# The MLP's three products by Strassen's scheme of seven half products, in a two-block transformer kernel

## The chip, the cores and the metric

One Trainium2 chip, one core of it, all numbers in float32. The time is the device time of one execution, in microseconds; each kernel is compared by the median of its runs. The engines are called PE (matrix products; PEld is its weight loads), DVE, ACT, POOL (elementwise work) and SP (here only the issue of DMAs).

## What is computed

Two blocks over x of 32 sequences x 64 tokens x 512 channels, conditioned on one vector of 512 per sequence:

```
block 0: h = rms(x) * (w1 * (1 + cond @ tw1.T));   q, k, v = h @ Wq.T, h @ Wk.T, h @ Wv.T   (8 heads of 64, one k and v)
         x += softmax(rope(q) rope(k).T / 8) v @ Wo.T
         h = rms(x) * (w2 * (1 + cond @ tw2.T))
         x += (silu(h @ Wg.T) * (h @ Wu.T)) @ Wd.T          Wg, Wu: 2048 x 512, Wd: 512 x 2048
block 1: h = layernorm(x) * (1 + scale) + shift;  q = h @ Wq.T (16 heads of 32);  c = h @ Wkd.T (128)
         k, v = c @ Wku.T, c @ Wvu.T (4 groups);   x += softmax(masked rope(q) rope(k).T / sqrt(32)) v @ Wo.T
```

The change concerns the line with Wg, Wu and Wd.

## The kernel before

All activations lie transposed: 128 channels on the partitions, tokens in the free dimension. The 2048 tokens are cut into 8 units of 256 (4 sequences). A unit passes through `attention0` (first block's attention and the norm for the MLP), `mlp`, and `attention1` (the whole second block, which also writes the result). `mlp(g)` works on a group of two units, 512 tokens. It loops over 16 blocks f of 128 hidden channels: 4 matmuls for gate, 4 for up (line 687, each 128x128 weights by 512 columns), Silu on ACT (692), the product `act` on DVE (695), and one block later 4 matmuls of down into four banks (678). At the end DVE adds the four banks to x (704). The weights of a block f (gate, up and down, 768 KB) come by one DMA into one of four `mw` buffers and are loaded anew in each of the four groups; `load_chunks` asks for block f + 4 when down has used block f.

Each of these functions is a Python generator. It yields after every piece with two numbers, a guess of PE's time and of the time until its next piece can go on. `Order.run` picks, among the jobs that can go on, the one with the least share done, so that attention's pieces stand between the MLP's in PE's instruction stream; a list scheduler then fixes the order on each engine. Every engine works its own stream in order and waits there by semaphores, SP's stream of DMA issues too. While `mlp(g)` runs, attention0 of the next two units and attention1 of earlier ones are interleaved. The last two units' attention1 run at the end, with every PSUM bank to themselves. PSUM has eight banks of 512 columns: two `at` for attention, two `gu` for gate and up, four `acc` for down.

Other steps that are spoken of: `rotate` (371 to 374, rotary embedding: three DVE products, one POOL addition), `softmax` (381 to 388), `turned` (394, transposes on PE), `inverse_root` (332 and 333: Sqrt on ACT, reciprocal on DVE), `rms` (324, 325 and 349 on POOL), `angles` (253 to 282, positions to sines and cosines on DVE).

Of the kernel before, what the change touches and what calls it, by code (L numbers as in the profile page):

```python
# [10 lines left out]
F32 = mybir.dt.float32  # L11
# [13 lines left out]
GT = 512  # L25
NG = T // GT
FF = 2048
NF = FF // P
# [64 lines left out]
def two_blocks(ctx: ExitStack, tc: tile.TileContext, a: dict, out: bass.AP):  # L93
# [3 lines left out]
    wk = ctx.enter_context(tc.tile_pool(name="wk", bufs=2))  # L97
    psum = ctx.enter_context(tc.tile_pool(name="psum", bufs=2, space=PSUM))
# [69 lines left out]
    XB = NU - 1  # L168
# [7 lines left out]
    chunks = {}  # L176

    def load_chunks(upto):

        for j in range(len(chunks), min(upto, NG * NF)):  # L180
            t = work("mw", [P, 3, 512], f"mw_{j}", MW)
            nc.sync.dma_start(t, a["wmlp"][j % NF])
            chunks[j] = t
# [3 lines left out]
    def load_mod(i):  # L187

        if i < 2:
            t = work("h2", [P, KC, D], f"mod_{i}", 2)  # L190
            nc.sync.dma_start(t, a["mod"][i])
            mods.append([t[:, :, c * P : (c + 1) * P] for c in range(KC)])
            return
        mods.append([])
        for j in range(2):
            t = work("mw", [P, KC, D // 2], f"mod_{i}_{j}", MW)
            nc.sync.dma_start(t, a["mod"][i][:, :, j * 256 : (j + 1) * 256])
            mods[i] += [t[:, :, c * P : (c + 1) * P] for c in range(2)]
# [3 lines left out]
    posi = work("pT", [P, GT], "posi", 3).bitcast(I32)  # L202
    nc.sync.dma_start(posi, a["pos"])
# [4 lines left out]
    load_mod(2)  # L208
    load_mod(3)
    load_x(2)  # L210
    load_x(3)


    def modulation(i):
# [12 lines left out]
        rows = work("latT", [P, UT], f"rows_{i}", 1)[:, :P]  # L227
# [16 lines left out]
    def angles(u0, u1):  # L244
        cols = slice(u0 * S, u1 * S)

        def room(tag, name, bufs):
            return work(tag, [P, 512], f"{name}_{u0}", bufs)[:, : (u1 - u0) * S]

        posf, sign = room("u", "posf", 2), room("v", "sign", 2)  # L250
        ang, lo, hi, prod = (room("p", n, 4) for n in ("ang", "lo", "hi", "prod"))
        acc, rnd = angle[:, 0, cols], angle[:, 1, cols]
        nc.vector.tensor_copy(posf, posi[:, cols])
# [28 lines left out]
        nc.vector.tensor_tensor(rnd, rnd, sign, ALU.mult)  # L282

    def tables(u, r):
# [6 lines left out]
        cs = work("cs", [P, 2, UT], f"cs_{u}", 2)  # L291
# [17 lines left out]
    RING = {"h": 4, "p": 4, "pT": 3, "sq": 1, "latT": 1, "kr": 1}  # L309

    def space(room, tag, columns, name):

        if room is not None and tag in room:
            return room[tag].pop(0)[:, :columns]
        return work(tag, [P, columns], f"{name}", RING.get(tag, 2))

    def mean_of(t, lean, name):

        if lean:
            ps = abank(name)  # L320
            for k in range(KC):
                nc.tensor.matmul(ps[:, :UT], ones, t[:, k], start=(k == 0), stop=(k == KC - 1))
        else:
            nc.gpsimd.tensor_tensor(t[:, 0:2], t[:, 0:2], t[:, 2:4], ALU.add)
            nc.gpsimd.tensor_tensor(t[:, 0], t[:, 0], t[:, 1], ALU.add)
            yield 0.0, 3.5
            ps = abank(name)
            nc.tensor.matmul(ps[:, :UT], ones, t[:, 0], start=True, stop=True)
        return ps[:, :UT]
# [5 lines left out]
    def rms(u, s, h, lean, name):  # L335

        x = x_units[u]
        sq = work("h" if lean else "sq", [P, KC, UT], f"sq_{name}", 4 if lean else 1)
        nc.scalar.activation(sq, x, AF.Square)
        if lean:  # L340
            c = KC // 2
# [6 lines left out]
        else:  # L348
            nc.gpsimd.tensor_tensor(by_seq(h), by_seq(x), per_seq(s, u), ALU.mult)  # L349
        ps = yield from mean_of(sq, lean, f"ms_{name}")  # L350
        r = work("r", [P, UT], f"r_{name}", 2)
        inverse_root(ps, eps0, r)
# [6 lines left out]
    def rotate(dst, src, cos, sin, shape, name, room=None):  # L359
# [4 lines left out]
        u, v = (space(room, tag, 512, f"{tag}_{name}") for tag in "uv")  # L364
# [11 lines left out]
    def softmax(sc, scale, name, p):  # L376
# [3 lines left out]
        mx = work("mx", [P, 8], f"mx_{name}", 3)  # L380
# [4 lines left out]
        sm = work("sm", [P, 8], f"sm_{name}", 3)  # L385
# [26 lines left out]
    h2s = {}  # L412

    def attention0(u, lean=False, early=None):
        g = u // 2
        half = slice((u % 2) * UT, (u % 2 + 1) * UT)
        kb, vb = kblk0[u % 2], vblk0[u % 2]
        h = work("h", [P, KC, UT], f"h0_{u}", 4)
        norm = rms(u, s0a, h, lean, f"a{u}")
# [8 lines left out]
        qT = work("qT", [P, KC, UT], f"qT0_{u}", 2)  # L428
# [55 lines left out]
        for t in range(2):  # L484
# [12 lines left out]
            ps.append(softmax(sc, HD0**-0.5, f"0_{u}_{t}", space(None, "p", 512, f"p0_{u}_{t}")))  # L497
            yield 1.0, 5.0 * t

        cT = work("h", [P, KC, UT], f"cT0_{u}", 4)  # L500
        for t in range(2):
            pT = turned(ps[t], f"0_{u}_{t}", space(None, "pT", 512, f"pT0_{u}_{t}")).rearrange("p (c t) -> p c t", c=KC)
# [17 lines left out]
        if u % 2 == 0:  # L520
            h2s[g] = work("h2", [P, KC, GT], f"h2_{g}", 2)
        h = h2s[g][:, :, half]
        r = yield from rms(u, s0b, h, lean, f"b{u}")
        nc.vector.tensor_tensor(h, h, all_chunks(r), ALU.mult)  # L524
        yield 0.43, 0.0


    def attention1(u, room=None):
        vb = room["vb"] if room else vblk1[u % 2]
        x = x_units[u]  # L530
        lean = room is not None and "h" in room

        def tile4(tag, name):
            return space(room, tag, KC * UT, name).rearrange("p (c t) -> p c t", t=UT)

        h = tile4("h", f"h1_{u}")
        if lean:
            mean = yield from mean_of(x, True, f"mean_{u}")
        else:
            sums = tile4("sq", f"sum_{u}")  # L540
            nc.gpsimd.tensor_tensor(sums[:, 0:2], x[:, 0:2], x[:, 2:4], ALU.add)
            nc.gpsimd.tensor_tensor(sums[:, 0], sums[:, 0], sums[:, 1], ALU.add)
            yield 0.0, 3.5
            mean = abank(f"mean_{u}")[:, :UT]
            nc.tensor.matmul(mean, ones, sums[:, 0], start=True, stop=True)
        nc.vector.tensor_tensor(h, x, all_chunks(mean), ALU.subtract)
        sq = tile4("sq", f"sq1_{u}")
        nc.scalar.activation(sq, h, AF.Square)  # L548
        nc.gpsimd.tensor_tensor(by_seq(h), by_seq(h), per_seq(s1, u), ALU.mult)  # L549
        yield 0.43, 3.0  # L550
        var = yield from mean_of(sq, lean, f"var_{u}")
        r = space(room, "r", UT, f"r_c{u}")
        inverse_root(var, eps1, r)
# [10 lines left out]
        qT = tile4("qT", f"qT1_{u}")  # L564
        cos, sin = cs1[:, 0, :], cs1[:, 1, :]

        def query(i):
            q = abank(f"q1_{u}_{i}")
            for c in range(2):
# [9 lines left out]
                room,  # L579
# [7 lines left out]
        for t in range(2):  # L587
# [12 lines left out]
            room,  # L600
        )
        kb = space(room, "kb1", KC * UT, f"kb1_{u}").rearrange("p (b g s) -> p b g s", b=US, g=NKV1)
# [16 lines left out]
        cT = tile4("h", f"cT1_{u}")  # L619
# [51 lines left out]
    def mlp(g):  # L671
        h = h2s[g]
        accs = [bank("acc", f"down_{g}_{c}") for c in range(KC)]

        def down(f, act):
            w = chunks[g * NF + f][:, 2]
            for c in range(KC):
                nc.tensor.matmul(accs[c], w[:, c * P : (c + 1) * P], act, start=(f == 0), stop=(f == NF - 1))  # L678
            load_chunks(g * NF + f + 1 + MW)

        before = None
        for f in range(NF):
            w = chunks[g * NF + f]
            gate, up = bank("gu", f"gate_{g}_{f}"), bank("gu", f"up_{g}_{f}")
            for ps, i in ((gate, 0), (up, 1)):
                for k in range(KC):
                    nc.tensor.matmul(  # L687
                        ps, w[:, i, k * P : (k + 1) * P], h[:, k, :], start=(k == 0), stop=(k == KC - 1)
                    )
                if i == 0:  # L690
                    sg = work("sg", [P, GT], f"sg_{g}_{f}", 2)
                    nc.scalar.activation(sg, gate, AF.Silu)  # L692
                yield 3.4, 0.0
            act = work("act", [P, GT], f"act_{g}_{f}", 3)
            nc.vector.tensor_tensor(act, sg, up, ALU.mult)  # L695
            if before is not None:
                down(*before)
                yield 3.4, 0.0
            before = f, act
        down(*before)  # L700
        for i in range(2):
            x = x_units[2 * g + i]
            for c in range(KC):
                nc.vector.tensor_tensor(x[:, c], x[:, c], accs[c][:, i * UT : (i + 1) * UT], ALU.add)
        yield 3.4, 0.0


    A0, A1, M = 24.0, 24.0, 164.0
    order = Order()

    def first(u, rank=0):
        return Job(attention0(u), A0, rank)

    def second(u, rank=0):
        return Job(attention1(u), A1, rank)

    def other_mods():
        for i in range(1, 4):
            yield from modulation(i)

    def after(*jobs):

        for j in jobs:
            yield from j

    def early():
        angles(0, 2)
        for z in (kblk0[0], vblk0[0], kblk0[1], vblk0[1], *vblk1):
            nc.gpsimd.memset(z, 0.0)
# [129 lines left out]
```

## Time and profile before

| | |
|---|---|
| median of 3 runs | 1123.04 us (1122.53 to 1123.87) |
| profiled execution | 1121.74 us, its span 1119.9 us |
| mean granted PE clock | 0.986 of full speed |
| first MLP matmul | 95.1 us after the span's start |
| last MLP matmul | 1011.6 us |
| PE / DVE / ACT / POOL busy | 96 / 36 / 24 / 20 % of the span |
| DMA | 68.8 MB, 61 GB/s on average |

The span is the time between the first and the last instruction. A line of the groups reads: source line, engine, operation, what is written from what, shapes and count, then busy time in us, mean duration in ns, and after the second bar the engine's idle time just before and what ended it. A matmul's duration is its latency from start to result; matmuls in a row overlap, so its price on PE is the distance between two starts. In the timeline the columns are start, time until the last of the merged instructions ended, engine, line, operation, and count.

### The profile page before, as it was taken

To read this page: it belongs to the slowest core of one execution; us is meant where nothing else is said; L and a number is where in the kernel's file an instruction comes from. 1 tells how busy PE (TensorE), PEld (TensorE's weight loads), DVE (VectorE), ACT (ScalarE), POOL (GpSimd) and SP (SyncE) were. 2 spreads that over 40 slices of the span, in tenths; PEclk is the share of its full clock that TensorE was granted. 3 is DMA by queue.
4 is the path that set the end of the run, shared out by engine and by line. 5 is a ranking of instruction groups with operands and counts; after the bars stand their busy time and mean duration, and the time that the engine had idled before them with its cause. 6 is when DMAs were issued, how large, how long until landed. Compare 5 with 4: busy or idle time off the path is not lost.

```text
span 1119.9 us, 10307 instructions
## 1 busy us (share of the span) xinstructions
PE 1079.6 (96%) x4100; PEld 631.6 (56%) x4100; DVE 407.2 (36%) x722; ACT 266.5 (24%) x441; POOL 226.5 (20%) x197
## 2 busy tenths in 40 slices
PE   6789999999999999999999999999999999999796
PEld 5575455645464645465565655555554555546584
DVE  5884111432252144332433224322233023115543
ACT  2231021121212142412114221243023023113222
POOL 2311012111132120202322212202131022014431
PEclk9899999999999999999999999999999999999898
DMA  9500211111201111112101121101111111200000
GB/s 363 220 1 1 85 56 57 57 57 56 85 29 56 57 57 57 57 65 84 59 28 57 37 67 57 57 29 66 66 57 57 75 56 57 75 1 0 1 30 29
DMA packets 16271, 68.83 MB, mean 61 GB/s; under 512 B 1632, under 2 KB 3936, under 8 KB 15456
## 3 DMA queue, kind: packets, MB, share of 16 engines
q1 hardware_dynamic: 16224, 68.17, 17.3%
q8 instruction: 33, 0.54, 0.2%
q14 instruction: 14, 0.11, 0.0%
HBM read 63.97 MB, written 4.19 MB: 61 GB/s over the span
## 4 chain that ended last, share of the span: by engine, by line
PE 89%; DVE 7%; POOL 1%; issue 1%; ACT 1%; DMA 0%; SPq 0%; ACTq 0%; DVEq 0%; POOLq 0%
PE down L678 20%; PE gate L687 19%; PE up L687 19%; PE po L357 9%; PE q L357 8%; PE sc L625 2%; PE pp L394 2%; PE cx L646 1%; PE lat L357 1%; PE sc L490 1%; PE cx L506 1%; PE kv L357 1%; PE tab L288 1%; DVE mx L381 1%; DMA mod<-in_mod 0%
## 5 line engine op out<-in xcount | busy, mean ns | idle before, releaser
L687 PE MATMUL up<-h,mw 128*128 128x512 f32 x512 | 232.8, 595 | 0.0
L678 PE MATMUL down<-act,mw 128*128 128x512 f32 x512 | 232.2, 595 | 0.0
L687 PE MATMUL gate<-h,mw 128*128 128x512 f32 x512 | 231.6, 594 | 0.4 <-DVE h L524 0.4
L687 PEld LDWEIGHTS gate<-h,mw 128*128 128x128 f32 x512 | 95.8, 190 | 107.8 <-issue 105.5
L678 PEld LDWEIGHTS down<-act,mw 128*128 128x128 f32 x512 | 95.6, 190 | 107.3 <-issue 105.4
L687 PEld LDWEIGHTS up<-h,mw 128*128 128x128 f32 x512 | 95.2, 190 | 108.0 <-issue 107.0
L695 DVE TENSOR_TENSOR act<-sg,up 128x512 f32<-128x512 f32 x64 | 43.7, 682 | 291.3 <-PE up L687 282.3
L692 ACT ACTIVATE sg<-gate 128x512 f32<-128x512 f32 x64 | 38.2, 597 | 315.0 <-PE gate L687 276.0
L357 PE MATMUL po<-cT,wo 128*128 128x256 f32 x448 | 100.8, 379 | 0.7 <-ACT cT L515 0.7
L357 PEld LDWEIGHTS po<-cT,wo 128*128 128x128 f32 x448 | 84.9, 190 | 21.2 <-issue 9.5
L388 POOL TENSOR_TENSOR p<-p,sm 128x512 f32<-128x512 f32 x40 | 41.2, 1042 | 234.0 <-DVE sm L387 225.8
L374 POOL TENSOR_TENSOR qT<-u_q,v_q 128x512 f32<-128x512 f32 x28 | 35.5, 1267 | 170.9 <-DVE v_q L373 170.9
L407 DVE TENSOR_TENSOR x<-x,po 128x512 f32<-128x512 f32 x32 | 22.0, 687 | 117.4 <-PE po L357 117.4
L357 PE MATMUL q<-h,wqkv 128*128 128x256 f32 x256 | 59.6, 384 | 1.6 <-DVE h L346 1.6
L381 DVE TENSOR_REDUCE mx<-sc 128x8 f32<-128x512 f32 x48 | 32.8, 685 | 75.6 <-PE sc L625 53.6
L357 PEld LDWEIGHTS q<-h,wqkv 128*128 128x128 f32 x256 | 48.6, 192 | 12.3 <-issue 5.8
L692 ACT ACT_TABLE_LOAD x30 | 38.5, 1283 | 59.6 <-PE gate L687 59.4
L357 PE MATMUL q<-h,wq 128*128 128x256 f32 x192 | 43.5, 379 | 0.1
L357 PEld LDWEIGHTS q<-h,wq 128*128 128x128 f32 x192 | 36.3, 190 | 6.6 <-issue 1.7
L384 ACT ACTIVATE p<-p 128x512 f32<-128x512 f32 x40 | 24.8, 629 | 54.7 <-DVE p L383 54.6
L549 POOL TENSOR_TENSOR h<-h,s 128x1024 f32<-128x1024 f32 x6 | 11.4, 1901 | 123.5 <-ACT sq L548 123.5
L349 POOL TENSOR_TENSOR h<-x,s0b 128x1024 f32<-128x1024 f32 x6 | 11.4, 1902 | 122.8 <-DVE x L407 122.8
(190 smaller groups left out, 1038.9 us busy)
## 6 DMA issues: line engine op xcount, KB each, us to landing
mw<-in_wmlp SPq DMA_DIRECT2D x64, 768.0 KB, 4.3
x<-in_x SPq DMA_DIRECT2D x8, 512.0 KB, 9.4
out_x<-x SPq DMA_DIRECT2D x16, 256.0 KB, 2.0
mod<-in_mod SPq DMA_DIRECT2D x2, 1024.0 KB, 8.4
wo<-in_wo SPq DMA_DIRECT2D x2, 1024.0 KB, 13.0
mod<-in_mod SPq DMA_DIRECT2D x4, 512.0 KB, 14.4
wqkv<-in_wqkv SPq DMA_DIRECT2D x1, 1280.0 KB, 9.0
wq<-in_wq SPq DMA_DIRECT2D x1, 1024.0 KB, 11.4
```

Of the source, the lines that this page charges most:

```text
L357: nc.tensor.matmul(ps, w[:, k, cols], h[:, k, :], start=(k == 0), stop=(k == KC - 1))
L374: nc.gpsimd.tensor_tensor(dst, cut(u, every), cut(v, every), ALU.add)
L381: nc.vector.tensor_reduce(mx, s3, AX.X, ALU.max)
L384: nc.scalar.activation(p, p, AF.Exp, scale=scale)
L388: nc.gpsimd.tensor_tensor(p3, p3, sm.unsqueeze(2).to_broadcast(heads), ALU.mult)
L394: nc.tensor.transpose(pp[:, c, :], p[:, c * P : (c + 1) * P], ident)
L407: nc.vector.tensor_tensor(x[:, part], x[:, part], po, ALU.add)
L625: nc.tensor.matmul(sc[b * S : (b + 1) * S, j * 256 : (j + 1) * 256], qT[:, 2 * h_ + j, cols], kb[:, 2 * t + b].rearrange("p g k -> p (g k) ...
L678: nc.tensor.matmul(accs[c], w[:, c * P : (c + 1) * P], act, start=(f == 0), stop=(f == NF - 1))
L687: nc.tensor.matmul(ps, w[:, i, k * P : (k + 1) * P], h[:, k, :], start=(k == 0), stop=(k == KC - 1))
L692: nc.scalar.activation(sg, gate, AF.Silu)
L695: nc.vector.tensor_tensor(act, sg, up, ALU.mult)
```

## The change

A product C = A B is cut into a 2 x 2 grid of blocks on each side. Instead of eight block products, seven are formed of sums of blocks (Winograd's form of Strassen's scheme), and their sums give the four blocks of C.

- The MLP runs unit by unit (256 tokens, in halves of `HT` = 128), and over `NP` = 8 pairs of hidden blocks, 256 channels: 64 steps. In each step gate, up and down each form P1 to P7, of two 128x128 by 128-column matmuls.
- The weight side of one product is a set of seven slots of 128x256: three blocks as they are (slots 4 to 6) and four sums (slots 0 to 3). In the first unit `combine` forms the sums, three operations on POOL and one on DVE, and `done_with` stores them to `kept`, 24 tiles in HBM. In later units slots 0 to 3 are loaded from there. There are four set buffers; a set is loaded when the set four places before it is used up.
- The token side is formed on chip: `attention0` adds four DVE operations for sums of h (`hc`); `gated` forms act and its sums (`td`) on POOL.
- `first_products` puts four of the products into the quarters of one `gu` bank; ACT copies one out, DVE adds three times; `last_products` accumulates the other three on top of the quarters that were read, and DVE adds once more. Silu is made in two parts. For down the seven sums stand in the four `acc` banks over all eight steps, and are added to x at the unit's end.
- Buffers: 5 x tiles for 7; the attention's buffers in two named sets (`ring`); the smaller buffers shared or single; positions loaded two units at a time.
- The order: the MLP starts when unit 0 is ready; attention0 of the next unit and a chain of attention1 of units 0 to 5 run beside it; units 6 and 7 at the end.

The core of the diff:

```diff
+    OF = {"P1": (4, "B11"), "P6": (1, "T2"), "P5": (0, "T1"), "P7": (2, "T3")}
+    OF |= {"P2": (5, "B21"), "P3": (3, "B22"), "P4": (6, "T4")}
...
+            t = work("mw", [P, 7, 2 * P], f"set_{n}", MW)
+            nc.sync.dma_start(t[:, 4:7], a["wmlp"][i][:, 0:3])
+            if q < NP:
+                odd[n] = work("a21", [P, 2 * P], f"a21_{n}", 2)
+                nc.sync.dma_start(odd[n], a["wmlp"][i][:, 3])
+            else:
+                nc.sync.dma_start(t[:, 0:4], kept[i])
...
+            nc.gpsimd.tensor_tensor(t[:, 0], a21, t[:, 6], ALU.add)
+            nc.gpsimd.tensor_tensor(t[:, 1], t[:, 0], t[:, 4], ALU.subtract)
+            nc.vector.tensor_tensor(t[:, 2], t[:, 4], a21, ALU.subtract)
+            nc.gpsimd.tensor_tensor(t[:, 3], t[:, 5], t[:, 1], ALU.subtract)
...
+    def done_with(m, q):
+        n = place[m, q]
+        if q < NP:
+            nc.sync.dma_start(kept[3 * (q % NP) + m], sets[n][:, 0:4])
+        load_sets(n + 1 + MW)
...
+        nc.vector.tensor_tensor(t1_, b12, b11, ALU.subtract)
+        nc.vector.tensor_tensor(b12, b22, b12, ALU.subtract)
+        nc.vector.tensor_tensor(t2_, b22, t1_, ALU.subtract)
+        nc.vector.tensor_tensor(t4_, b21, t2_, ALU.subtract)
...
-            gate, up = bank("gu", f"gate_{g}_{f}"), bank("gu", f"up_{g}_{f}")
-            for ps, i in ((gate, 0), (up, 1)):
-                for k in range(KC):
-                    nc.tensor.matmul(
-                        ps, w[:, i, k * P : (k + 1) * P], h[:, k, :], start=(k == 0), stop=(k == KC - 1)
-                    )
...
+        for i, p in enumerate(("P1", "P6", "P5", "P7")):
+            product(ps[:, i], p, w, b, start=i == 0)
+        e = work("e", [P, HT], f"e_{m}_{q}")
+        nc.scalar.copy(e, ps[:, 0])
+        u2 = work("u2", [P, HT], f"u2_{m}_{q}")
+        nc.vector.tensor_tensor(u2, e, ps[:, 1], ALU.add)
+        w2 = work("w2", [P, HT], f"w2_{m}_{q}")
+        nc.vector.tensor_tensor(w2, u2, ps[:, 2], ALU.add)
+
+        c = work("gate" if m == 0 else "up", [P, 4, HT], f"c_{m}_{q}", 2 - m)
+        nc.vector.tensor_tensor(c[:, 2], w2, ps[:, 3], ALU.add)
...
+        for i, p in ((0, "P2"), (2, "P3"), (3, "P4")):
+            product(ps[:, i], p, w, b, stop=p == "P4")
+        nc.vector.tensor_tensor(
+            c.rearrange("p (a b) t -> p a b t", b=2)[:, :, 1],
+            ps[:, 2:4],
+            u2.unsqueeze(1).to_broadcast([P, 2, HT]),
+            ALU.add,
+        )
+        done_with(m, q)
...
+        nc.vector.tensor_tensor(act[:, 0], gate[:, 0], ps[:, 0], ALU.mult)
+        nc.gpsimd.tensor_tensor(act[:, 1:4], gate[:, 1:4], c[:, 1:4], ALU.mult)
+        td = work("td", [P, 4, HT], f"td_{q}")
+        nc.gpsimd.tensor_tensor(td[:, 0:2], act[:, 1:3], act[:, 0:2], ALU.subtract)
+        nc.gpsimd.tensor_tensor(td[:, 2], act[:, 2], td[:, 0], ALU.subtract)
+        nc.gpsimd.tensor_tensor(td[:, 3], act[:, 3], td[:, 2], ALU.subtract)
...
+            gate = first_products(0, q)
+            yield 1.8, 0.0
+            up = first_products(1, q)
+            yield 1.8, 0.0
+            before = down(q - 1) if q else iter(())
+            yield from before if q == 0 else (next(before),)
+            last_products(0, q, *gate)
+            nc.scalar.activation(gate[2][:, 0], gate[0][:, 0], AF.Silu)
+            nc.scalar.activation(gate[2][:, 1:4], gate[2][:, 1:4], AF.Silu)
+            yield 1.3, 0.0
+            last_products(1, q, *up)
+            gated(q, up[0], up[2], gate[2])
+            yield 1.3, 0.0
+            for _ in before:
+                pass
```

## The prediction, made before the changed kernel was run

> **What bounds the kernel now.** I read the page first: busy times, slices, the chain that ended last, the costliest groups and the DMA issues.
>
> ```profile
> span 1119.9 us, 10307 instructions
> ...
> PE 1079.6 (96%) x4100; PEld 631.6 (56%) x4100; DVE 407.2 (36%) x722; ACT 266.5 (24%) x441; POOL 226.5 (20%) x197
> ...
> PE 89%; DVE 7%; POOL 1%; issue 1%; ACT 1%; DMA 0%; SPq 0%; ACTq 0%; DVEq 0%; POOLq 0%
> ...
> L687 PE MATMUL up<-h,mw 128*128 128x512 f32 x512 | 232.8, 595 | 0.0
> L678 PE MATMUL down<-act,mw 128*128 128x512 f32 x512 | 232.2, 595 | 0.0
> L687 PE MATMUL gate<-h,mw 128*128 128x512 f32 x512 | 231.6, 594 | 0.4 <-DVE h L524 0.4
> ...
> mw<-in_wmlp SPq DMA_DIRECT2D x64, 768.0 KB, 4.3
> ```
>
> PE is 89% of the chain; the three MLP products have almost no idle time before them. Each 128-row product in float32 stands in the trace as two matmuls: 256 by the program per product, 512 by the profile. So PE's own time is what must shrink. "595" is one matmul's latency; the price is the distance from one start to the next, and the timeline gives it.
>
> ```profile
> 105.52 3.60 PE L687 MATMUL up<-h,mw 128*128 128x512 f32 x8
> 105.52 0.19 PEld L687 LDWEIGHTS up<-h,mw 128*128 128x128 f32 x1 [0.24 <-issue]
> ```
>
> Eight matmuls of 512 columns take (3.60 - 0.595)/7 = 0.429 us each; the weight load of 0.19 us hides under them. MLP now: 1536 x 0.429 = 659 us. The change makes columns few and loads many, so I looked for 128 columns with a new weight block each time.
>
> ```profile
> 66.96 1.04 PE L394 MATMUL pp<-ident,p 128*128 128x128 f32 x8
> ```
>
> ```profile
> 356.19 0.63 PEld L588 LDWEIGHTS kv<-wkv,latT 128*128 128x128 f32 x4
> 356.41 0.61 PE L588 MATMUL kv<-wkv,latT 128*128 128x128 f32 x4
> ```
>
> These come from the timeline; 0.273 and 0.275 are the latencies in the tiles' rows. The transposes: (1.04 - 0.273)/7 = 0.110 us. The kv product: (0.61 - 0.275)/3 = 0.112 us, its four loads starting at the same pace although each lasts 0.19 us. So loads follow one another at 0.11 us, and 128 columns cost just over a quarter of 512 (0.107).
>
> Last, from the groups by shape, POOL's and then DVE's, the prices of the engines that get new work (the number before the last bar is the mean in ns).
>
> ```profile
> L324 POOL TENSOR_TENSOR sq_b<-sq_b 128x512 f32<-128x512 f32 x6 | 7.6, 1265 | 0.0
> ...
> L325 POOL TENSOR_TENSOR sq_b<-sq_b 128x256 f32<-128x256 f32 x6 | 4.3, 723 | 0.5
> ```
>
> ```profile
> L704 DVE TENSOR_TENSOR x<-x,down 128x256 f32<-128x256 f32 x32 | 12.0, 418 | 4.8 <-PE down L678 3.6
> ...
> L264 DVE TENSOR_TENSOR prod<-prod,angle 128x128 f32<-128x128 f32 x16 | 4.7, 292 | 0.5
> ```
>
> **PE's work.** Per unit (256 tokens) and pair of blocks (a "step", 64 in all) there are 3 products x 7 half products x 2 matmuls = 42, in the trace 84. All: 64 x 84 = 5376. At 0.110 that is 591 us, at 0.112 602; I take 0.111: 597, a gain of 62 us (57 to 68). A step is 84 x 0.111 = 9.32 us in six pieces: gate's and up's first four products (1.78 each), down's first four of the step before (1.78), then gate's, up's and down's last three (1.33 each).
>
> The Trainium skill, page "TensorE: Matmul & The Clock Gate", section "Back-to-back issue gap", speaks against this: streams of load and matmul at 128 columns are paced at about 81 ns where the matmul alone would take about 56. Scaling 0.110 by 81/56, an estimate from that page, makes MLP 855 us and the kernel about 1346. The rows above, with a new weight block for every matmul, show no such factor; no row here shows more than eight in a row.
>
> **Evictions, units 1 to 7.** MLP's 0.68 us DVE product per f goes (64, 44 us). A step gets on DVE seven operations of 128 columns (0.29) and two of 256 (0.42): 2.9 us, 184 us in all; DVE comes to some 570 of 1090 us, not a bound. ACT gets two small copies and the Silu in two parts, about 1.3 us a step, plus six table loads by the order of instructions (79 for 73, 1.28 us each); off the path. POOL gets act (384 columns, 0.99 between its 256 and 512 rows) and td (0.72 + 2 x 0.45): 2.6 us, 167 in all.
> What counts is each wait of PE against its cover:
> - Gate's last products need four readings of its first (copy 0.27, three adds 0.87, hand-overs and matmul latency 0.4): 1.55 us; up's and down's first products cover 3.56. Up's: the same 1.55 under 3.11.
> - Down needs act and td: latency and add 0.7, POOL until the second operand of down 1.0 + 0.72 + 0.45: 2.9 us, under down's rest, gate's and up's first products, 4.89.
> - The gate and up banks come free in 0.7 to 1.0 us, under 2.67 and 3.11.
> So alone nothing shows. Attention's operations stand in the same queues: on DVE runs of 2 us (rotate, three at 0.69) to 4.7 (reciprocal of line 333 1.75, h of line 524 1.28, four new sums at 0.42), on ACT a table load and Exp, on POOL 1.0 (line 388) to 1.9 (line 349) each. They use up the spare 1.5 to 2 us, but bring PE work that widens it: before, MLP ran from 95 to 1012 us, 917 us with 659 of MLP, so 258 of attention (about 4 us a step). I take 0.2 us a step: 56 x 0.2 = 11 us. Below: zero. Above: 1.65 us a step, see the slower rival.
>
> **Unit 0, where sums are made.** Here POOL also has three operations of 256 columns for each of three sets a step: 9 x 0.723 = 6.5, with act and td 9.1 us beside PE's 9.32, and hardly any attention widens it (only the rest of unit 1's first block). Its queue takes act and td first (0.6 for the add and hand-overs, then 2.6), then up's, down's, gate's sums. The next up's second product needs two sums (2 x 0.723 = 1.45): they end 3.2 + 1.45 = 4.7 us after the last up, PE is there after 1.33 + 1.78 + 0.44 = 3.55; so it waits 1.15, and down's sums add some 0.35. So 1.5 us x 8 = 12 us. SP adds a queue of its own: a set's load waits behind the store of the previous set's sums, and that behind POOL. Below: 0, if the order turns out kinder. Above: DMA's price, next. From the timeline of POOL and then of DVE, a contended operation (start, duration):
>
> ```profile
> 525.97 1.67 POOL L325 TENSOR_TENSOR sq_a<-sq_a 128x256 f32<-128x256 f32 x1
> ```
>
> ```profile
> 525.85 1.21 DVE L524 TENSOR_TENSOR h<-h,r_b 128x1024 f32<-128x1024 f32 x1
> ```
>
> 1.67 for 0.72, beside a DVE operation with both inputs in SBUF. DVE's slot 2 of each set is of that kind.
>
> **DMA.** Before, 64 loads of 0.79 MB. Now a set is 0.92 MB (0.39 weights, 0.52 kept sums), three a step: 2.75 MB; in unit 0 loads of 0.52 and stores of 0.52, 3.15 MB. Four buffers: up's set is asked for when gate's is used up, 4.4 us of PE work ahead, down's 6.2, gate's 12. The window 20 to 30 us moved 396 GB/s:
>
> ```profile
> 20.00:30.00 10.00, 10.00 (x64) 8.62 (x57) 7.70 (x23) 3.21 (x5) 1.17 (x1) 1.00 1.06 396
> ```
>
> At that rate 2.75 MB take 6.9 us of a 13 us step: hidden; the first product of a set uses raw weights, so kept sums may land 0.45 later. At the lone load's 0.79 MB in 4.3 us (183 GB/s, nothing overlapped) a step takes 15 us, 1.7 more than the 13.3 there is: 95 us over 56 steps, and in unit 0 17.2 us for 9.3, 63 us. The three loads are asked for within 2.7 us of one another, like the window's queued loads, so I take the upper rate and nothing beyond unit 0's 12. SP's two loads a set cost 0.33 us each of issue (one x load's issue in the timeline); behind out_x and the three later x loads sets can wait 2.0 us (out_x's landing): 0 to 6, taken as 0.
>
> **Boundaries, head, end.** Eight units instead of four groups: four evictions of DVE and the four sums end later than PE wants; 7 x 0.7 = 5 us (0 to 20). MLP starts after one unit, near 75 us instead of 95, but the attention work that stood there comes later: 0 (-5 to +5). The end keeps two and a half second blocks: 0 (-5 to +5).
>
> **The sum**, against the profiled execution's 1121.7 us (span 1119.9 and 1.8 around it): -62 + 11 + 12 + 5 = -34, so 1087.7. That execution lies 1.3 below the median of 1123.0; added, 1089.
>
> **Rivals.**
> *All hidden.* No wait is added: 1123 - 68 = 1055 to 1061. For it: every cover above exceeds its chain. Against: unit 0's POOL is full.
> *Slower: POOL's queue.* Place: down's wait for td. Attention has about 170 us of POOL in MLP's stretch, 2.7 us a step; with one h operation of 1.9 that itself waits for a reciprocal of 1.75, the chain of 2.9 grows to 6.55 and misses 4.89 by 1.66: 56 x 1.65 = 92, with the 17 of unit 0 and the boundaries 1123 - 62 + 92 + 17 = 1170. It decides from 45/56 = 0.8 us a step with the other terms as they are. Against: attention's PE work widens 4.9 to about 7.
> *Loads pace PE.* If a long stream needed the whole 0.19 of a load, MLP takes 1021 us and the kernel 1485; the 0.11 pace of four loads speaks against it.
>
> **Chances.** Forecast, waits of 15 to 50 us in all, so 1076 to 1111: 0.52. All hidden: 0.26. POOL's queue, in any strength: 0.19 (of it 0.14 past the break-even). Loads: 0.03. What this kernel's measurement can tell from no change is 0.2%, 2.2 us. Faster 0.79, within 0.04, slower 0.17. The range 1054 to 1140 leaves out the worst of POOL's queue and the loads.
>
> **What would show it.** In the profile after: 128-column MLP matmuls, eight or more together, at 0.110 to 0.112; if nearer 0.19, I am wrong at the root. PE's idle time in unit 0 about 12 us, released by POOL's sums or DMA; afterwards short waits of down for td and of last products for DVE adds. If SPq or DMA releases PE in units 1 to 7, the lone rate was right. If PE idles over 60 us in all that the before does not have, it is slower.

## The result, and the profile after

The changed kernel takes 1128.11 us (median of 4 runs, 1127.75 to 1129.35), the kernel before 1122.78 in the same comparison: ratio 1.0050, 95% interval 1.0032 to 1.0067. It is slower by half a percent, where 3% less was forecast. The page of the changed kernel, busy times, chain and the MLP's groups:

```profile
span 1126.0 us, 20184 instructions
...
PE 1045.3 (93%) x7940; PEld 954.6 (85%) x7940; DVE 577.9 (51%) x1314; ACT 317.6 (28%) x647; POOL 471.2 (42%) x557
...
PE 69%; DVE 11%; POOL 7%; DMA 5%; ACT 3%; issue 2%; SPq 0%; POOLq 0%; ACTq 0%; DVEq 0%
...
L719 PE MATMUL gu<-h,set 128*128 128x128 f32 x2048 | 293.4, 278 | 9.8 <-ACT c L814 3.7
...
L719 PE MATMUL gu<-hc,set 128*128 128x128 f32 x1536 | 217.0, 277 | 11.9 <-POOL set L212 7.8
...
L778 PE MATMUL down<-td,set 128*128 128x128 f32 x1024 | 137.4, 277 | 5.9 <-POOL set L212 3.3
```

PE fell from 96 to 93% busy, its share of the chain from 89 to 69%: DVE, POOL and DMA took the rest. The MLP's groups had next to no idle time before them; now they have. PE's waits, from the view of waits (us in all, times, longest):

```profile
PE lat L400 <- POOL h L599: 9.9, 5, 4.6
PE pp L437 <- POOL p L431: 9.0, 8, 6.7
PE gu L719 <- POOL set L212: 7.8, 6, 1.6
PE tab L325 <- DVE angle L317: 7.4, 3, 4.1
...
PE gu L719 <- ACT c L814: 3.7, 5, 1.5
PE gu L719 <- DVE hc L570: 3.3, 4, 1.4
PE down L778 <- POOL set L212: 3.3, 4, 2.0
PE gu L719 <- DVE c L738: 2.6, 3, 1.2
```

No wait dominates; it is a long list, and that view leaves short ones out. So for all kernels I also added up, from the trace, the distance from each matmul's start to the next beyond what its columns take when nothing waits (0.109 us for 128 columns, 0.216 for 256, 0.429 for 512). "Head" is before the first MLP matmul, "tail" after the last, both without the time before PE's first matmul; a constant excess below 0.01 us a matmul, 13 us in all at 128 columns, is kept apart. The kernels below "changed" are the experiments of the next section.

| kernel | median us | ratio to before, 95% | head | unit 0 | units 1 to 7 | tail |
|---|---|---|---|---|---|---|
| before | 1122.8 | | 24.8 | 13.9 for all units | | 25.8 |
| changed | 1128.1 | 1.0032 to 1.0067 | 30.3 | 23.0 | 60.2 | 16.9 |
| conv | 1129.2 | 1.0049 to 1.0086 | 25.8 | 0.0 | 28.0 | 13.1 |
| convcut | 1052.8 | 0.9341 to 0.9396 | 26.2 | 0.0 | 35.0 | 15.4 |
| bare | 1092.7 | 0.9718 to 0.9747 | 26.8 | 5.3 | 45.0 | 17.2 |
| nosum | 1109.1 | 0.9865 to 0.9916 | 26.7 | 7.9 | 59.6 | 17.3 |
| nodma | 1121.4 | 0.9988 to 1.0012 | 31.2 | 22.2 | 56.1 | 17.3 |
| notd | 1121.8 | 0.9966 to 1.0020 | 28.1 | 19.0 | 55.4 | 17.3 |
| noadd | 1133.4 | 1.0063 to 1.0148 | 28.9 | 20.6 | 69.4 | 20.1 |
| noangle | 1120.6 | 0.9962 to 1.0009 | 29.0 | 23.8 | 53.7 | 17.3 |
| ownsilu | 1127.9 | 1.0027 to 1.0067 | 28.8 | 24.1 | 63.8 | 17.3 |
| lag | 1123.6 | 1.0000 to 1.0018 | 27.6 | 26.0 | 56.5 | 17.0 |
| tddve | 1118.4 | 0.9968 to 1.0004 | 28.2 | 17.9 | 53.5 | 17.0 |
| tddvelag | 1118.4 | 0.9931 to 0.9989 | 30.5 | 16.5 | 57.8 | 17.3 |
| plain0 | 1134.9 | 1.0104 to 1.0161 | 27.9 | 19.1 | 65.4 | 20.1 |
| plain0b | 1129.8 | 1.0044 to 1.0075 | 27.7 | 13.3 | 64.1 | 16.8 |
| combo | 1118.3 | 0.9956 to 0.9985 | 27.2 | 12.4 | 55.8 | 16.9 |
| store | 1136.6 | 1.0075 to 1.0146 | 31.9 | 28.2 | 60.7 | 17.3 |
| best2 | 1127.6 | 1.0022 to 1.0055 | 34.0 | 24.9 | 56.6 | 16.9 |
| dvesum | 1109.4 | 0.9863 to 0.9903 | 27.6 | 10.0 | 53.4 | 17.3 |

Waits are those of one profiled execution, and executions of several kernels differ by up to 12 us, so a difference of a few us between two rows of waits says little. The kernel before took 1121.1 to 1122.8 us beside the several experiments, so medians of two rows can differ by 1 to 2 us for nothing. From before to changed: products 659 to 600.6, so 58 us less, and waits 64.5 to 130.4, so 66 more. That is the result: the products shrank as forecast, and PE stood still for all of it and a little more.

### The profile page after: what moved, and what is told of

The parts are those of the page before. It is cut to its first block, busy times and chain, and to the rows that moved or that the text cites. A ratio compares the mean times of both kernels' runs of the same rounds, so it can differ in the third digit from the quotient of the medians.

```text
span 1126.0 us, 20184 instructions
## 1 busy us (share of the span) xinstructions
PE 1045.3 (93%) x7940; PEld 954.6 (85%) x7940; DVE 577.9 (51%) x1314; ACT 317.6 (28%) x647; POOL 471.2 (42%) x557
## 4 chain that ended last, share of the span: by engine, by line
PE 69%; DVE 11%; POOL 7%; DMA 5%; ACT 3%; issue 2%; SPq 0%; POOLq 0%; ACTq 0%; DVEq 0%
PE gu L719 25%; PE down L778 13%; PE po L400 10%; PE q L400 8%; DMA set<-sums 3%; DMA set<-in_wmlp 2%; PE sc L667 2%; PE lat L400 2%; PE pp L437 2%; PE cx L547 1%; PE kv L400 1%; PE sc L531 1%; PE cx L688 1%; POOL set L212 1%; POOL set L211 1%
## 5 line engine op out<-in xcount | busy, mean ns | idle before, releaser
L719 PE MATMUL gu<-h,set 128*128 128x128 f32 x2048 | 293.4, 278 | 9.8 <-ACT c L814 3.7
L719 PEld LDWEIGHTS gu<-h,set 128*128 128x128 f32 x2048 | 262.2, 193 | 23.0 <-issue 11.3
L719 PE MATMUL gu<-hc,set 128*128 128x128 f32 x1536 | 217.0, 277 | 11.9 <-POOL set L212 7.8
L719 PEld LDWEIGHTS gu<-hc,set 128*128 128x128 f32 x1536 | 194.0, 193 | 15.2 <-POOL set L212 8.9
L757 POOL TENSOR_TENSOR act<-c,c 128x384 f32<-128x384 f32 x64 | 65.0, 1015 | 218.0 <-DVE c L745 174.5
L778 PE MATMUL down<-td,set 128*128 128x128 f32 x1024 | 137.4, 277 | 5.9 <-POOL set L212 3.3
L778 PEld LDWEIGHTS down<-td,set 128*128 128x128 f32 x1024 | 125.2, 192 | 9.4 <-POOL set L212 4.1
L778 PE MATMUL down<-act,set 128*128 128x128 f32 x768 | 110.2, 278 | 1.0 <-DMA set<-in_wmlp 0.8
L745 DVE TENSOR_TENSOR c<-gu,u 128x256 f32<-128x256 f32 x128 | 53.5, 421 | 112.0 <-PE gu L719 111.0
L778 PEld LDWEIGHTS down<-act,set 128*128 128x128 f32 x768 | 98.7, 193 | 7.6 <-issue 3.6
```

Of the source, the lines that this page charges most:

```text
L719: nc.tensor.matmul(ps, w[:, slot, k * P : (k + 1) * P], b[of][:, k], start=start and k == 0, stop=k == 1, skip_group_check=True)
L745: nc.vector.tensor_tensor(c.rearrange("p (a b) t -> p a b t", b=2)[:, :, 1], ps[:, 2:4], u2.unsqueeze(1).to_broadcast([P, 2, HT]), ALU.add,)
L757: nc.gpsimd.tensor_tensor(act[:, 1:4], gate[:, 1:4], c[:, 1:4], ALU.mult)
L778: nc.tensor.matmul(sums_of[u][p][:, c], w[:, slot, c * P : (c + 1) * P], b[of], start=q % NP == 0 and i % 2 == 0 and c == 0, stop=q % NP = ...
```

## The experiments

The edits are shown shortened.

### What each part of the change is worth

**conv**: the changed kernel's units, buffers and order, with plain products and plain evictions. **nosum**: no sums of weights formed or stored.

```diff
+ for r in range(2): for k in range(KC): matmul(ps[:, r], w[:, SLOT[r, k // 2], ...], h[:, k, :])     # conv
+ activation(sg, gate, Silu); tensor_tensor(act, sg, up, mult)
+ nc.sync.dma_start(t[:, 0:4], a["wmlp"][i])                                                          # nosum
- combine(...); dma_start(kept[...], sets[n][:, 0:4])
```

> The changed kernel's frame (units of 256 tokens, its order, its buffers, its set loads) with plain products of 256 columns: no sums, no evictions by quarters. MLP's products cost 64 x 48 x 0.216 = 663 us for 602, so +61 at equal waits. Theory A (the waits come from the elementwise work that Strassen adds): the waits of units 1 to 7 fall from 60 to 15 to 25 us and those of unit 0 from 23 to under 5, in all about -60: 1120 to 1135 us. Rival C (they come from the rest of the change: order by unit, single buffers): the waits stay, 1165 us or more. Rival B (late sets): the loads are 0.52 MB for 0.92, so this one does not tell B from A.

> Leaves out the forming and storing of the sums: slots 0 to 3 are loaded from the weights in every unit, so the values are others; every other instruction stays. Theory A: unit 0's waits of 23 us, released by POOL's sums, go; about 1128 - 20 = 1108, units 1 to 7 unchanged within 4 us. Rival B (DMA): unit 0 now loads 0.92 MB a set as the others do, waits stay near 15 to 20 us, released by DMA: 1122 or more.

**bare** takes away, beyond nosum, the elementwise operations that the scheme adds in every step. What stays of the scheme are the sets of 0.92 MB (conv's are 0.52) and, at the end of each unit, down's sums (one operation on ACT, seven on DVE, four on POOL, where conv has four on DVE). **convcut** takes one matmul of eight from conv.

```diff
- u2, w2, c, hc and td sums, second Silu                     # bare, on top of nosum
+ activation(gate[2], gate[0], Silu); tensor_tensor(act, gate, ps, mult)
- for k in range(KC):                                        # convcut, on top of conv
+ for k in range(KC - r):
```

> Seven half products in the same order as in the changed kernel, but none of the elementwise work that the scheme adds: no sums of weights (all sets are loaded), of tokens or of act, and gate and up are evicted as plain ones are, one Silu and one product of the whole bank (the outputs are not the reference's). It stands against the kernel without sums of weights, 1109.1. Theory A (the added elementwise work makes the waits): units 1 to 7 fall from 60 us of waits to the 28 of plain products, unit 0 from 8 to 0: 1109 - 40 = 1069 (1062 to 1078). Theory D (PE has less MLP work to cover attention's chains, whatever stands beside it): waits stay, 1095 to 1108.

> Plain products and plain evictions in the changed kernel's frame, with one of eight matmuls of every block left out (the outputs are not the reference's): 663 x 1/8 = 83 us less MLP work on PE and nothing added elsewhere; it stands against plain products, 1129.2. Theory A: the waits stay near the 28 us of plain products: 1129 - 83 = 1046 (1042 to 1054). Theory D: with less to lay under attention's chains PE waits 25 to 40 us more in units 1 to 7: 1070 to 1086. Between them: both count.

Measured: conv 1129.2 and nosum 1109.1, both where theory A had them, bare 1092.7, convcut 1052.8. In a line from before to changed this is the whole account:

- 1122.8 to 1129.2 (conv): the new frame alone, +6.4.
- to 1092.7 (bare): seven half products for eight, with the larger sets and down's sums at the units' ends, -36.5. The products themselves shrank by 63 (664 to 601), waits took 27 back: 5 in unit 0, 17 in units 1 to 7, 5 in head and tail.
- to 1109.1 (nosum): the sums of tokens and act and the split evictions, +16.4; of it 15 in units 1 to 7.
- to 1128.1 (changed): forming and storing the sums of weights, +19.0; of it 15 in unit 0 and 4 in the head.

Bare fell between the two theories (1062 to 1078, 1095 to 1108). Of its waits in units 1 to 7 these six lead:

```profile
PE tab L318 <- DVE angle L310: 4.9, 1, 4.9
PE lat L393 <- POOL h L587: 3.1, 2, 2.8
PE gu L707 <- DMA set<-in_wmlp: 2.4, 3, 1.1
PE pp L430 <- POOL p L424: 2.1, 4, 0.8
PE var L361 <- POOL tot_v L354: 2.0, 2, 1.8
PE down L747 <- DMA set<-in_wmlp: 1.6, 4, 0.5
```

With DVE 39% and POOL 23% busy, PE still comes to steps of attention before their chains are through: 13.1 us in this view, for 8.1 in conv and 10.1 in convcut. It waits 4.0 us for the sets' loads, and 3.2 in unit 0; conv and convcut have no such wait. So of the 17 us that units 1 to 7 wait more than in conv, attention's chains are 5, the loads 4, and the other 8 this view does not place.

Convcut says how far less cover alone does this: with 83 us of matmuls gone the time fell by 76.4, so 7 us came back as waits (28.0 to 35.0). By the view of waits 2 of them are attention's; most of the rest is clock: in units 1 to 7 of its profile PE's clock stands at half for 13.7 us, in conv's for 3.4, which costs half of the difference, 5 us (the last section shows what sets this off). The time is within theory A's range; but A fails on bare: without the added work of the steps 45 us of waits remain. About 10 us, bare's 45.0 against convcut's 35.0, belong to what bare has beyond convcut: the form of the seven products, the larger sets, down's sums. The loads are 4 us of it by the view; no run takes the three apart.

### Which of the added operations

**nodma**: units 1 to 7 load only the raw quarters, 0.39 MB for 0.92. **notd**: no sums of act. **noadd**: two of DVE's four additions left out.

```diff
- nc.sync.dma_start(t[:, 0:4], kept[i])                      # nodma
+ slot = 4 + slot % 3 if late else slot
- nc.gpsimd.tensor_tensor(td[:, 0:2], ...), (td[:, 2], ...), (td[:, 3], ...)      # notd
- nc.vector.tensor_tensor(u2, e, ps[:, 1], ALU.add); (w2, u2, ps[:, 2], ...)      # noadd
```

> Leaves out the loading of the kept sums in units 1 to 7 (88 of 197 MB); the products read the raw slots there, so the values are others. Rival B (PE waits for sets, or SP's queue is full): the waits of units 1 to 7 fall from 60 to under 30, 1095 to 1105 us. Theory A: only the 5 us go that PE waited for DMA: 1120 to 1128.

> Leaves out the three POOL operations td of every step (1.64 us a step, 105 us of POOL); down reads plain quarters of act, so the values are others. If POOL's queue is the one that makes PE wait (the slower rival of the prediction): -30 or more, 1098 or less. Theory A with the load spread over DVE, ACT and POOL: -8 to -20, 1108 to 1120. If only DVE's evictions matter: 1123 to 1128.

> Two of DVE's four additions after the first products of gate and up are left out (the outputs are not the reference's): 128 x 2 x 0.285 = 73 us less on DVE, and each last product of gate and up may start 0.57 us earlier. Theory A with DVE as the engine that counts: a third to a half of the 32 us that units 1 to 7 wait more than with plain products: 1112 to 1118, 3 us of it in unit 0. Rival (POOL's act, td and sums make the waits): 1124 to 1128. Rival (PE waits for the banks, whatever DVE has to do): 1126 to 1128.

By their ratios against the changed kernel's 1.0050, nodma gains 0.5% (6 us), notd 0.6% (6 us): neither the transfers nor down's wait for td is the main cost. Noadd, with DVE busy 511 us for 578, gains nothing (1.0063 to 1.0148). These additions of DVE were covered, as the prediction had it; my expectation of 10 to 16 us was wrong.

**noangle**: the angles of units 2 to 7 copied from units 0 and 1 (other than its expectation says, the copies are the right angles here: the positions of all sequences are equal; only this input allows it). **ownsilu**: the Silu of the first quarter into its own tile, for which w2 has one buffer instead of two. **lag**: more room in the written order.

```diff
+ if u0: nc.vector.tensor_copy(angle[:, :, cols], angle[:, :, 0 : 2 * S]); return      # noangle
- nc.scalar.activation(gate[2][:, 0], gate[0][:, 0], AF.Silu)                          # ownsilu
+ nc.scalar.activation(g0, gate[0][:, 0], AF.Silu)
- job.ready = self.now + latency                                                       # lag
+ job.ready = self.now + 1.5 * latency
```

> The angles of units 2 to 7 are copied from those of units 0 and 1 (the outputs are not the reference's): three times some 38 DVE operations of 0.3 to 0.4 us and two of ACT are left out, 40 us of DVE's 578, all of it during units 1, 3 and 5. Theory A with DVE's load as the cause: these units wait like the even ones, 13 us each less 8: 15 us less, about 1113 (1110 to 1118). If DVE has room for the angles and the odd units wait for another reason: 1125 to 1129.

> The Silu of the quarter that stays in the bank goes into a tile of its own, so ACT need not wait for DVE's last addition into the other quarters before it frees the gate's bank; the result is the same. Theory (the shared tile makes PE wait for ACT when the next gate's first products want the bank): the 3.7 us that PE waits for this Silu go, and part of the 4.5 us between down's last and gate's first products: 1122 to 1125. Rival (the bank would come free too late anyway, or the wait moves to DVE's additions): 1126 to 1129.

> The order written at build time keeps every operation; only the times that it leaves to an attention step's chain on DVE, ACT and POOL before it queues the next PE work of that step are 1.5 times as long while the eight units run (5.5 becomes 8.25 us, and so on). Theory D (PE now has 63 us less MLP work between the attention steps while their chains carry more DVE and POOL work, so PE reaches an attention step before its operand): the waits of over 0.2 us in units 1 to 7, 35 us against 9.5 with plain products, lose those at lat, var, tab, pp and ms (13 us): 1115 to 1122. Rival (these are the chains' own length, put off but not covered, and given back at the units' ends or in the tail): 1125 to 1133.

Noangle gained 7.5 us, half of what was expected; units 3 and 5 waited 10.0 and 8.6 for 12.2 and 13.3. Ownsilu gained nothing: PE's wait for that Silu stayed at 3.7 us in 5 waits, so what ACT waited for in that tile was not what held the bank. Lag gained 4.5 us: the waits of lat and tab fell from 17.3 to 8.4, those for the sets' loads rose from 5 to 15. So part of the waits of units 1 to 7 is attention's chains coming late, but the order can't hide much of it.

### DVE and POOL beside each other

**tddve**: act and td on DVE.

```diff
- nc.gpsimd.tensor_tensor(act[:, 1:4], ...); nc.gpsimd.tensor_tensor(td[...], ...) x3
+ nc.vector.tensor_tensor(act[:, 1:4], ...); nc.vector.tensor_tensor(td[...], ...) x3
```

> act's three quarters and td's three operations go from POOL to DVE, the result is the same: POOL loses 172 us (64 x 2.68), DVE gains about 100 (64 x 1.55 by its rows of 128 and 256 columns). If POOL's queue and the lengthening of operations when both engines work on SBUF make the waits: about 6 us less as with td left out, 1118 to 1123. If DVE's load makes them: 100 us more on DVE at the price that the angles seem to have (15 us for 40): 1140 to 1165. If neither: 1126 to 1130.

It gained 9.7 us though DVE rose from 578 to 679 us busy: 100 us more on the busier engine made the kernel faster. One reason shows in the lengths of DVE's own operations. In the changed kernel's timeline (start, duration):

```profile
678.57 1.04 POOL L757 TENSOR_TENSOR act<-c,c 128x384 f32<-128x384 f32 x1 [9.47 <-DVE c L745]
678.68 1.22 DVE L570 TENSOR_TENSOR hc<-h,hc 128x256 f32<-128x256 f32 x1
...
679.95 1.16 PE L719 MATMUL gu<-hc,set 128*128 128x128 f32 x8 [1.36 <-DVE hc L570]
...
680.99 2.08 POOL L594 TENSOR_TENSOR h<-h,s 128x1024 f32<-128x1024 f32 x1
681.23 1.92 DVE L303 TENSOR_SCALAR prod<-hi 128x128 f32<-128x128 f32 x1
```

An operation of 0.42 us takes 1.22 beside POOL, and PE waits 1.36 for it. The groups by shape, of the changed kernel and then of tddve, say the same of all eight of them (mean ns before the last bar):

```profile
L570 DVE TENSOR_TENSOR hc<-h,hc 128x256 f32<-128x256 f32 x8 | 5.7, 714 | 0.0
```

```profile
L570 DVE TENSOR_TENSOR hc<-h,hc 128x256 f32<-128x256 f32 x8 | 3.4, 420 | 0.0
```

The additions of `angles` (line 309) took 405 ns, in tddve 310, in conv 291. The Trainium skill, page "SBUF — State Buffer", section "SBUF: two separate sides", says that DVE, where both of its inputs lie in SBUF (against a POOL operation that reads SBUF) or it runs in a two-port mode, and POOL hold one pair of ports in turn for a whole instruction. The rows agree: the operation beside POOL lasts its own 0.42 us plus most of POOL's 1.04; additions with an input in PSUM kept their 285 ns.

How much of the 9.7 us this makes no run shows. A rival stands beside it: without act and td in its queue POOL also comes to unit 0's sums earlier. There PE's waits for POOL's second sum fell from 11.1 to 8.6 us; in all unit 0 lost 5 us of waits, units 1 to 7 lost 7.

### Unit 0

**plain0** and **plain0b**: unit 0 with plain products while the sums are formed beside them; plain0b without the two small buffers for the fourth quarter.

```diff
+ if u == 0: yield from mlp_plain(); return                                     # plain0
- nc.sync.dma_start(odd[n], a["wmlp"][i][:, 3])                                 # plain0b
+ nc.sync.dma_start(t[:, 3], a["wmlp"][i][:, 3])
+ nc.gpsimd.tensor_tensor(t[:, 3], t[:, 5], t[:, 1], ALU.subtract)  # after the products
```

> Unit 0 alone takes plain products (256 columns, raw weights); the sums of weights are still formed and stored beside them and read by units 1 to 7. Theory A (elementwise work that Strassen's scheme adds, standing in chains that PE waits for): unit 0's waits fall from 23.0 us to the 0 to 2 us of the kernel with plain products everywhere, its products cost 7.9 us more (63 us of products saved over eight units, one eighth), the four sums of the tokens go from the head (-2): about 1128 - 23 + 8 = 1112 (1107 to 1117). Rival (forming the sums loads POOL, DVE and the stores whatever reads them, so the attention work beside it and the late sets cost the same): 1126 to 1136.

> As the kernel with plain products in unit 0, but the fourth quarter of the weights is loaded into the place of the fourth sum, which is formed after the products have used it, so no product waits for the two small buffers of that quarter (10.7 + 1.8 us of waits there). Theory A: unit 0's waits 2 to 8 us for 23.0, its products +8.5 us: 1128 - 18 + 8.5 = 1118 (1113 to 1122). Rival (forming the sums and storing them holds back the sets whatever reads them): the waits for set loads stay at 12 us or more, 1126 to 1136.

Plain0 ran into its own fault: plain products read those two buffers, and PE waited 10.7 us for them. Plain0b's unit 0 waits 13.3 for 23.0 and pays 8.5 for its products; of the waits 9.5 are down's for a set's load. The times of both lie in their rival's range.

**combo** joins tddve, ownsilu, plain0b and lag; **tddvelag** tddve and lag.

> All four exact changes together: act and td on DVE, the Silu's own tile, plain products in unit 0 with the sums beside them, the longer lags. If each removes waits of its own (-9.7 measured for the first, -4, -10 and -8 expected): 1096, faster than both kernels. If they remove the same waits or one puts them elsewhere: 1108 to 1118. If POOL, DVE and their lags are not the cause: 1120 or more.

> act and td on DVE and the longer lags together, the result is the same. If they remove waits of their own: 1118.4 - 4.5 = 1114 (1111 to 1117), faster than the kernel before. If the longer lags only move waits to the sets' loads, which then come due earlier: 1117 to 1122.

They gave 1118.3 and 1118.4, no less than tddve alone: the gains overlap. Both beat the kernel before, by 0.3 and 0.4%.

**store**: the sums' stores issued by POOL, off SP's queue. **best2**: store with tddvelag.

```diff
+ nc.gpsimd.dma_start(kept[3 * q + m], t[:, 0:4])     # at the end of combine
- nc.sync.dma_start(kept[3 * (q % NP) + m], sets[n][:, 0:4])
```

> The stores of the sums are issued by POOL straight after the fourth sum, not by SP when the set is used up; the result is the same. If unit 0's waits come from loads that stand behind stores on SP's queue: about half of its 23 us, 1114 to 1120. If POOL's pace is what counts, the issue on its queue adds to it: 1126 to 1136.

> act and td on DVE, the longer lags and the stores issued by POOL; the result is the same. With waits of its own removed by each: 1118 less 6 to 10, 1108 to 1112, faster than both kernels. If POOL, freed of act and td, already hides the queue: 1115 to 1120.

Slower by 8.5 and 9 us than the same kernels without it. POOL's queue carries each issue (store, the number before the last bar is the mean in ns):

```profile
L216 POOL DMA_DIRECT2D sums<-set x24 | 14.0, 584 | 6.6 <-POOL set L214 4.2 <-DVE set L213 2.1 <-issue 0.4
```

In unit 0 of store PE's waits for POOL's second sum rose from 11.1 to 13.8 us, and those for loads, which a freer SP should have cut, from 1.8 to 3.9. This points to POOL's pace, not to SP's queue, though the run changes both at once. **dvesum** tests it from the other side: tddvelag with the first of the three sums on DVE.

```diff
- nc.gpsimd.tensor_tensor(t[:, 0], a21, t[:, 6], ALU.add)
+ nc.vector.tensor_tensor(t[:, 0], a21, t[:, 6], ALU.add)
```

> act and td on DVE, the longer lags, and of POOL's three sums of weights the first goes to DVE too, so each engine forms two; the result is the same. POOL loses 24 x 0.79 = 19 us in unit 0, DVE gains 24 x 0.42 = 10. If POOL's pace in unit 0 is what counts (two sums in a row of 0.8 us before P5 may start): unit 0's waits fall from 16.5 to about 9, 1118.4 - 7 = 1111 (1108 to 1115), faster than both kernels. If the sets' loads now come last: 1116 to 1121. If DVE, which waits for the sets' loads with the evictions queued behind, becomes the late one: 1121 to 1128.

1109.39 us (1104.82 to 1111.18), ratio 0.9883, interval 0.9863 to 0.9903: 9 us less than tddvelag, unit 0's waits 16.5 to 10.0, and 1.2% faster than the kernel before. The page of dvesum:

```profile
PE 1041.6 (94%) x7940; PEld 952.4 (86%) x7940; DVE 676.6 (61%) x1594; ACT 315.1 (29%) x645; POOL 289.9 (26%) x277
```

PE's waits for POOL's second sum in unit 0, first of tddvelag, then of dvesum:

```profile
PE gu L719 <- POOL set L212: 4.6, 5, 1.4
PE down L778 <- POOL set L212: 3.2, 4, 2.0
```

```profile
PE gu L719 <- POOL set L212: 2.8, 4, 0.7
...
PE down L778 <- POOL set L212: 0.4, 1, 0.4
```

They fell from 7.8 to 3.2 us; in the changed kernel they were 11.1 (7.8 and 3.3). The windows of unit 0, of the changed kernel, tddvelag and dvesum (length, then busy time and count of PE, PEld, DVE, ACT, POOL, then clock, DMA share, GB/s):

```profile
81.60:192.00 110.40, 96.27 (x735) 91.78 (x735) 52.36 (x137) 15.01 (x40) 70.23 (x95) 0.95 0.64 214
```

```profile
81.60:185.50 103.90, 92.86 (x735) 88.55 (x734) 61.60 (x169) 15.11 (x40) 50.35 (x63) 0.98 0.66 227
```

```profile
78.60:175.70 97.10, 90.53 (x733) 86.77 (x733) 67.70 (x185) 15.21 (x40) 33.72 (x41) 1.00 0.72 243
```

POOL goes from 64 to 48 to 35% of the unit, DVE from 47 to 59 to 70, and the unit takes 6.5, then 6.8 us less.

## Why the prediction was wrong, by its own steps

- **PE's work: the price held, its worth did not.** In a long row of the changed kernel's timeline

```profile
680.94 1.06 PE L719 MATMUL gu<-h,set 128*128 128x128 f32 x8
```

 eight take (1.06 - 0.278)/7 = 0.112 us each, the upper end of 0.110 to 0.112; the MLP is 600.6 us for a forecast 597. The factor 81/56 from the Trainium skill, page "TensorE: Matmul & The Clock Gate", section "Back-to-back issue gap", does not appear, over 5376 matmuls. But the sum let all of -62 through to the time. Run alone (conv to bare) the scheme gave -36.5. This is the step that failed most, 26 us: the prediction asked of each new wait whether it was covered, and never asked what PE's MLP work had been covering. What attention's chains and the sets' loads would cost when that cover shrank was no part of the sum. Of the 27 us of waits that bare has and conv has not, the view of waits puts 7 on the sets' loads and 5 on attention's chains in units 1 to 7; 5 are in head and tail, the rest it does not place. That less cover alone makes waits convcut shows, 7 us of them with plain products; for the whole 27 it is not shown.
- **Evictions, units 1 to 7: 11 forecast.** Measured 16.4 with unit 0's share (bare to nosum), 15 in units 1 to 7. A term somewhat too small. The covers as listed mostly held: leaving out two of DVE's four additions gains nothing (noadd), leaving out td 6 us. What was missed is that POOL's act and td lengthen DVE's operations that read SBUF, though no run shows how much of the 16.4 this is. The prediction showed such a pair (1.21 and 1.67 us side by side) and used it for unit 0 alone.
- **Unit 0: 12 forecast**, 19.0 measured (nosum to changed): 15 in unit 0, the rest mostly in the head, where the first sets are summed. The mechanism was right: PE's second product waits for POOL's two sums, 11.1 us in the view of waits. Its size missed the clock: three stretches at half clock, 5.1 us, and sums of 0.79 and 0.82 us for 0.72.
- **DMA: 0 forecast**, 6 us measured with nodma. The upper rate was near the truth; the lone rate's 95 us far off, although DMA does release PE in units 1 to 7 (3.4 us in the list), which the prediction had named as the lone rate's sign. Its lead times were too long: it counted all three sets from the moment gate's is used up, but by the kernel's order down's load is asked for when up's is, 4.9 us of PE work ahead and not 6.2, gate's 9.3 and not 12. The loads of sums landed 5.7 us after their issue (median).
- **Boundaries 5, head and end 0.** Conv's whole frame costs 6.4, right in size by luck: its units wait 14 us more than before and its products take 5 more, its tail waits 13 less. In the changed kernel the head's waits rose by 5.5 us, the tail's fell by 9, with 66 us of matmuls in it for 78.
- **The slower rival** named the wrong place. Down's wait for POOL's td is 0.4 us in the list and 6 us by notd, not 92. Slower came by many small waits, which no rival had.
- **The sign that was named came true**: "if PE idles over 60 us in all that the before does not have, it is slower". It was 66.

The working sum, in the prediction's terms: -62, +11, +12, +5 = -34 was, as measured, -36.5, +16.4, +19.0, +6.4 = +5.3. What stays open is why 27 us of waits came back in bare: no run took its loads, down's sums at the units' ends and the form of the products apart.

## What to carry to other kernels

When the engine that is 96% busy gets less work, its work was also the cover of everything beside it: price the saved time by a run that only leaves work out (here 83 us of matmuls gave 76, and the scheme's 63, with its larger loads, gave 36) before adding up what the new scheme costs. New elementwise work may belong on the busier engine, if that keeps it from meeting another engine on the same memory ports and shortens the queue that PE waits for: act and td on DVE, the sums split two and two, and the longer lags turned 1128 into 1109 us. And a wait is read as a place in one stage: to shorten unit 0's waits for POOL's sums, ten of about 1 us each, by one operation of three gained 9 us, to leave out all the loads of sums in units 1 to 7 gained 6.

## What the runs showed of the hardware

The clock reacts to half-empty windows, not only to idle ones. Two pairs of windows of the changed kernel, each of 3.4 us (clock is the number before the DMA share):

```profile
114.09:117.50 3.41, 1.21 (x9) 0.85 (x7) 1.26 (x4) 0.27 (x1) 2.60 (x4) 1.00 0.62 243
```

```profile
117.50:120.91 3.41, 3.21 (x15) 3.22 (x16) 0.99 (x3) 0.19 (x1) 3.17 (x6) 0.50 0.57 199
120.91:124.32 3.41, 3.41 (x32) 3.41 (x32) 1.20 (x4) 0.07 (x1) 2.04 (x3) 1.00 0.77 270
127.70:131.10 3.40, 1.61 (x13) 1.26 (x12) 1.54 (x5) 0.27 (x1) 3.04 (x5) 1.00 0.56 184
131.10:134.50 3.40, 3.40 (x18) 3.40 (x18) 0.51 (x2) 0.27 (x1) 3.24 (x5) 0.50 0.63 220
```

After a window in which PE is busy for 1.2 or 1.6 of 3.4 us the next one runs at half clock: 15 to 18 matmuls in it, where the window at full clock has 32. Between 85 and 1030 us, in the profiles of all twenty kernels of the table, a window at full clock with PE busy for under 43% of it was always followed by one at half clock, one with over 53% never, and in between both were seen. So a wait of 2 us can cost 1.7 more, half of such a window. The changed kernel has four such windows in its MLP stretch, three of them in unit 0, the kernel before none, dvesum one.

The Trainium skill, page "TensorE: Matmul & The Clock Gate", section "What's actually happening", has a window of about 3.4 us, half clock after an idle window and full clock after a busy one; the rows agree on the window and the two clocks, and differ in that a window need not be idle.
